# First block of each second pass: two products ahead of the last scores, the others in the usual order; joined with a new division of the W_lin sums and an earlier load of the last stored sum

## The chip, the cores and the metric

One core of a Trainium2 chip runs the whole kernel. The metric is the device time of one execution in microseconds (us), lower is better. The engines are TensorE (PE in the profile; its weight loads are PEld), VectorE (DVE), ScalarE (ACT), GpSimd (POOL) and SyncE (SP), which issues most of the DMAs, one after the other in program order.

## The reference

A pre-normalised graph network of two layers on 128 graphs of 64 nodes with 768 features, all in float32, with a residual around it. Cut to what matters:

```
h = relu(layernorm(x))                        # x: 128 x 64 x 768, adj: 128 x 64 x 64
for l in range(2):
    u_left  = (h @ (h @ W_left[l].T).T)  / sqrt(768)      # per graph
    u_right = (h @ (h @ W_right[l].T).T) / sqrt(768)
    u = upper triangle and diagonal of u_left, lower triangle of u_right
    e = exp(u) * adj
    attention = e / (sum(e, axis=2) + 1e-10)
    h_lin = h @ W_lin[l].T + b_lin[l]
    ctx = attention @ h_lin
    h = relu((ctx - mean) / (std + 0.001) * ln_a[l] + ln_b[l])
out = x + h
```

## The kernel before

The 8192 tokens are kept transposed (`ht`: features on partitions). Each layer has two passes over all of them.

**Pass one** makes the scores. The products of a 768x768 weight with tokens are made by a fast scheme: 40 products (`PRODUCTS`, L705) in place of more plain ones, each of a sum of weight blocks (a tile `g`, a "form") with a sum of token blocks (also `g`, or `ht` itself). One product is eight matmuls of 128x256 on PE. It writes one of the PSUM banks C, D, X, Y, Z, V, and is then read with signs into the results m0, m1, m2: the first read into a result is an ACT copy (L925), the others are DVE additions (L248, L929; L248 is the helper `added`). The tokens go by superblocks (`SUPER`, 11 per layer), and the 40 products are repeated for each. POOL makes the token sums (L248, `g<-ht`, `g<-ht,g`) a few products ahead; PE waits where one is late. After the fourth product of a superblock stand the scores of the superblock before (`scores`, L743), 288 short matmuls. The weight sums of layer 1 are formed during layer 0, stored to DRAM (`form`) and loaded in layer 1 (L654, `g<-form`).

**The plan.** What other engines do beside the products is written into a plan of slots: `put(slot, f)` enters a function, `turn_of(slot)`, called twice per product, runs what is due. The order of the code is the order in each engine's queue, and so one late instruction holds up what stands behind it. Beside the last superblock runs `final`: it loads the nine blocks of W_lin, centres them over the outputs (sums on ACT L236, means on DVE L231 and L232, the subtraction on ACT L240), does the same with the bias (`bias`: L983, L991, L994, L995, L998), and forms the 17 further weight sums of pass two (`W_SUMS`, by `sums_n`), by turns on POOL and DVE.

**Pass two** makes h_lin in 16 blocks with 15 products each (`ORDER`, L1021), into the banks Z, V, X, Y. `fresh` takes a bank and for four of the products writes the bias into it first (an ACT copy, L1010), `multiply` is the product, and a bank is read into h_lin (`hl`) by ACT (L303) or DVE. Of the first block the products 0 and 1 stand ahead of the scores of the last superblock of pass one; 3 and 5 come directly behind these, and then the others of the block in their order. Then follow the context (attention times h_lin, L1063, into `aux`), and from it a tile `z` (ACT L1208, L1226) that is normalised and stored for the next layer (`z<-z`). Of layer 0 there are four `z` buffers.

**The joint of the layers.** Layer 1 loads rows of z (`x<-z`, L364), transposes them by way of `xb` and `h` in DRAM, and loads `ht<-h` (L371). Those loads, the stored weight sums and the scores' own transfers all pass SyncE's one queue.

Of the kernel before, what the change touches and what calls it, by code (L numbers as in the profile page):

```python
# [10 lines left out]
F32 = mybir.dt.float32  # L11
I32 = mybir.dt.int32
AF = mybir.ActivationFunctionType
# [4 lines left out]
def kernel(  # L18
# [12 lines left out]
    nc = tc.nc  # L31
# [35 lines left out]
    def put(slot, *fs):  # L67
        plan.setdefault(slot, []).extend(fs)
# [12 lines left out]
    def run(slot):  # L81
# [7 lines left out]
        if background:  # L89
# [2 lines left out]

    SRC = {"l": w_left, "r": w_right, "n": w_lin}
    RAW = {8: (0, 1), 12: (1, 1), 9: (2, 1), 13: (2, 0), 11: (0, 0), 6: (1, 0), 3: (0, 2), 10: (1, 2), 14: (2, 2)}
    W_SUMS = ((5, "+", 8, 12), (9, "+", 9, 8), (8, "+", 8, 13), (0, "+", 5, 13), (4, "+", 3, 10),
# [3 lines left out]

    T_SUMS = (("ta", "+", "B0", "B2"), ("u1", "-", "B3", "B2"), ("u2", "-", "u1", "B0"), ("u0", "-", "B5", "B4"),  # L100
              ("u3", "-", "B1", "u0"), ("td", "+", "B3", "B4"), ("tb", "-", "B5", "B1"), ("te", "-", "B0", "u3"),
# [78 lines left out]
    def begins(k, l=0):  # L180
        return 0 if k == 0 else 2 * (len(PRODUCTS) if l else PLAIN) + 2 * len(PRODUCTS) * (k - 1)
# [65 lines left out]
    def added(eng, o, sign, a, b):  # L247
        (eng.tensor_add if sign == "+" else eng.tensor_sub)(o, a, b)  # L248

    def sums_n(l):  # L250
        t = W[l, "n"]

        def one(n, o, s, a, b):
            if o not in t:
                t[o] = free.popleft()
            added((nc.gpsimd, nc.vector)[n % 2], t[o], s, t[a], t[b])

        return [lambda n=n, x=x: one(n, *x) for n, x in enumerate(W_SUMS)]

    def later(fs, apart):  # L260
        for f in fs:
# [396 lines left out]
    def pass_one(l, start, final):  # L658
        with tc.tile_pool(name=f"one{l}", bufs=2, reuse_waits="tile") as sp, \
# [200 lines left out]
            def prepare(b, slot, step=1):  # L860
                if (l, b) not in XR:
                    load_rows(l, b, sp)
                end = put_all(slot + 1, [f for f in transpose_rows(l, b, sp) if step > 1 or f is not None], 1)
                if b + 1 < NB and (l, b + 1) not in XR:
                    if l == 0 and b > 2:
                        put(end - 5, lambda: load_rows(l, b + 1, sp, (0,)))
                        put(end, lambda: load_rows(l, b + 1, sp, (1,)))
                    else:
                        put(end + (8 if b == 2 else 0), lambda: load_rows(l, b + 1, sp))
                for t in range(2):  # L870
                    p = 2 * b + t
                    k = where[p][0]
                    before = p - 6
                    at = end + 3 + t
                    lag = 22 if b > 2 else 30 if l else 16
                    if before >= 0:
                        at = max(at, begins(where[before][0] + 1, l) + 2 * SCORED + 3)
                    put(at, lambda p=p, hold=before >= 0: load_part(1, l, p, hold))
                    put_all(at + lag + 6 * t, affine_part(1, l, p))
                    follow.setdefault(k, []).append(at + lag + (7 + 6 * t if l else 0))  # L880
                    if len(follow[k]) == len(SUPER[k]):
                        tokens.ready[k] = max(follow[k])
# [67 lines left out]
                    f()  # L950
            steps = softmax(last)
            steps[0]()
            for i in (0, 1, 3, 5):
                LEAD[i] = fresh(l, i, (0, 1))
                if i < 2:
                    multiply(l, 0, i, LEAD[i], (0, 1))
            scores(last)
            for i in (3, 5):
                multiply(l, 0, i, LEAD[i], (0, 1))
            for f in steps[1:4]:  # L960
                f()
            put_all(6, steps[4:], 3)
# [7 lines left out]
    def bias(l):  # L970


        ab = [free.popleft() for _ in range(2)]
        W[l, "bias"] = ab
        t = rows["bias", l] = [ab[n // 2][:, n % 2, :] for n in range(4)]
        todo = [lambda i=i, to=to: row(f"b{i}", b_lin[l], i * D, (i + 1) * D, t[to]) for i, to in enumerate((1, 2, 0))]
        bm = stat.tile([P, 3], F32, name="bm", bufs=1)

        bs = stat.tile([P, 1], F32, name="bs", bufs=1)

        def sums():
            for n in range(3):
                nc.scalar.activation(t[n], t[n], AF.Copy, accum_out=bm[:, n:n + 1])  # L983

        def mean():
            nc.vector.reduce_sum(bs, bm, axis=mybir.AxisListType.X)
            nc.vector.tensor_scalar_mul(bs, bs, -1.0 / H)

        def centred():
            for n in range(3):  # L990
                nc.scalar.activation(t[n], t[n], AF.Identity, bias=bs)  # L991

        def combined():
            nc.gpsimd.tensor_add(t[1], t[1], t[0])  # L994
            nc.gpsimd.tensor_add(t[3], t[1], t[2])  # L995

        def negated(n):
            nc.scalar.activation(t[n], t[n], AF.Copy, scale=-1.0)  # L998

        return todo, [sums, mean, centred, combined, lambda: negated(0), lambda: negated(2)]  # L1000
# [26 lines left out]
    def pass_two(l, aside):  # L1027
        last = l == L - 1
        with tc.tile_pool(name=f"two{l}", bufs=2, reuse_waits="tile") as sp, \
                tc.tile_pool(name=f"ps_two{l}", bufs=2, space=bass.MemoryType.PSUM, reuse_waits="tile") as ps_aux:  # L1030
            if last:
                for name, src in (("a", ln_a), ("b", ln_b)):
                    row(name, src[l], 0, H, sp.tile([P, H], F32, name=name, bufs=1))
            else:
                places(sp, {"hl": ([P, Q, H], 2), "at": ([P, Q, S], 2), "x": ([P, 2, H], 2),
                            "xb": ([P, H // 32, Q, 32], 1), "z": ([P, H], 4)}, ("hl", "at", "x", "xb", "z"))
            AT, HL = {}, {}
            if not last:
                extra = []
# [110 lines left out]
            def finish_block(u, more):  # L1150

                parts = context_block(u)
                tiles = ((0, 0), (0, 1), (1, 0), (1, 1))
                zs = {t: sp.tile([P, H], F32, name="z", bufs=4) for t in tiles}
                cut = (slice(0, T), slice(T, H))

                for t in ((1, 1), (1, 0)):
                    nc.vector.tensor_copy(zs[t][:, cut[0]], parts[t][0])
                    parts[t][0] = zs[t][:, cut[0]]
                    if t == (1, 1):  # L1160
                        AHEAD.append(fresh(l, 0, more))
                ss = stat.tile([P, Q, 2], F32, name="ssb", bufs=2)
                sd = stat.tile([P, Q], F32, name="sdb", bufs=2)
                rs = stat.tile([P, Q], F32, name="rsb", bufs=2)

                def squares(t):
                    junk = zs[0, t[1]]
                    for n in range(2):
                        nc.scalar.activation(junk[:, cut[n]], parts[t][n], AF.Square,
                                             accum_out=ss[:, 2 * t[0] + t[1], n:n + 1])  # L1170

                def deviation():
                    nc.vector.reduce_sum(sd, ss, axis=mybir.AxisListType.X)
                    nc.scalar.activation(sd, sd, AF.Sqrt, bias=floor, scale=1.0 / (H - 1.0))

                def inverse():
                    nc.vector.tensor_scalar_add(rs, sd, EPS_LN)
                    nc.vector.reciprocal(rs, rs)

                def scaled(t):  # L1180
                    by = rs[:, 2 * t[0] + t[1]:2 * t[0] + t[1] + 1]
                    for n in range(2):
                        nc.scalar.activation(zs[t][:, cut[n]], parts[t][n], AF.Copy, scale=by)
                    kept(u, *t, zs[t])

                order = ((1, 1), (1, 0), (0, 0), (0, 1))
                for f, slots in ((squares, (25, 26, 28, 29)), (scaled, (33, 34, 35, 36))):
                    for n, t in zip(slots, order):
                        put(n, lambda f=f, t=t: f(t))
                put(30, deviation)  # L1190
                put(32, inverse)
# [5 lines left out]
            def finish(u, r):  # L1197

                cx = context(u, r)
                zs = [sp.tile([P, H], F32, name="z", bufs=4) for _ in range(2)]  # L1200
                if last and not u and not r:
                    residual(u, r)
                two = "p (n d) -> p n d"
# [121 lines left out]
    def final_of(l):  # L1325
        def final(slot, tokens):
            put_all(slot + 6, load_n(l), 2)
            put(slot + 12, lambda: load_h(2, l, 0))

            def rest():  # L1330
                loads, work = bias(l)
                put_all(slot + 29, loads, 1)
                put_all(slot + 40, work, 4)

            put(slot + 28, rest)
            put_all(slot + 24, affine(2, l, 0), 2)
            put_all(slot + 28, centre(l), 1)
            for n, f in enumerate(sums_n(l)):
                put(slot + 42 + 3 * n // 2, f)
            put_sums_t((2, l, 0), slot + 56, 2, slot + 50)  # L1340
        return final

# [37 lines left out]
```

## Time and profile before

| | |
|---|---|
| median of 3 runs | 2643.37 us (2641.82 to 2644.38) |
| profiled execution | 2643.98 us |
| its span | 2642.2 us, 1.8 less |
| mean granted clock of PE | 0.996 |
| busy: PE, DVE, POOL, ACT | 98%, 67%, 67%, 35% |

The span is what the trace covers; all times of the trace count from its start. A row of the timeline has the start in us, the duration, engine, line, operation, the output and inputs by the program's names, and, in brackets, how long the engine sat idle just before and what ended that. A row of the stretches has start and end, then the busy time of each engine with its count of instructions, the granted clock of PE, the DMA share and the GB/s. Layer 0's pass one ends at about 860 us, layer 1's first pass begins at about 1330 and its second at about 2160.

### The profile page before, as it was taken

To read this page: it belongs to the slowest core of one execution; us is meant where nothing else is said; L and a number is where in the kernel's file an instruction comes from. 1 tells how busy PE (TensorE), PEld (TensorE's weight loads), DVE (VectorE), ACT (ScalarE), POOL (GpSimd) and SP (SyncE) were. 2 spreads that over 40 slices of the span, in tenths; PEclk is the share of its full clock that TensorE was granted. 3 is DMA by queue.
4 is the path that set the end of the run, shared out by engine and by line. 5 is a ranking of instruction groups with operands and counts; after the bars stand their busy time and mean duration, and the time that the engine had idled before them with its cause. 6 is when DMAs were issued, how large, how long until landed. Compare 5 with 4: busy or idle time off the path is not lost.

```text
span 2642.2 us, 47249 instructions
## 1 busy us (share of the span) xinstructions
PE 2590.5 (98%) x18122; PEld 2216.3 (84%) x18122; DVE 1776.0 (67%) x2884; ACT 934.9 (35%) x1969; POOL 1764.3 (67%) x1396
## 2 busy tenths in 40 slices
PE   9899999999999999999999999999999999999998
PEld 8788888888888888888788888888888878887886
DVE  6878787777768445454456677677766676666667
ACT  5522223223113344454542222222222335555453
POOL 4766676666668657676176666667666657878786
PEclk9999999999999999999999999999999999999999
DMA  7534434333421354445794524353542215555555
GB/s 219 115 109 98 113 93 125 92 106 79 98 57 60 123 164 142 159 144 183 218 279 96 126 59 113 76 129 93 131 104 70 66 50 160 156 166 167 176 161 146
DMA packets 258465, 331.84 MB, mean 126 GB/s; under 512 B 56002, under 2 KB 190402, under 8 KB 258242
## 3 DMA queue, kind: packets, MB, share of 16 engines
q1 hardware_dynamic: 241442, 320.56, 44.2%
q10 hardware_dynamic: 16800, 8.26, 1.2%
q8 instruction: 145, 2.38, 0.4%
q14 instruction: 78, 0.64, 0.1%
HBM read 213.39 MB, written 115.34 MB: 124 GB/s over the span
## 4 chain that ended last, share of the span: by engine, by line
PE 86%; DVE 5%; DMA 3%; ACT 2%; issue 1%; POOL 1%; SPq 1%; ACTq 0%; DVEq 0%; POOLq 0%
PE Z L1021 12%; PE C L705 8%; PE Y L705 8%; PE X L705 8%; PE D L705 8%; PE Y L1021 8%; PE Z L705 8%; PE V L705 7%; PE X L1021 6%; PE sc L743 5%; PE V L1021 4%; PE aux L1063 2%; DVE m L248 2%; POOL g L248 1%; DMA g<-form 1%
## 5 line engine op out<-in xcount | busy, mean ns | idle before, releaser
L248 POOL TENSOR_TENSOR g<-ht 128x512 f32<-128x512 f32 (+1 forms) x620 | 785.1, 1277 | 410.5 <-PE X L705 74.4
L248 POOL TENSOR_TENSOR g<-g,g 128x512 f32<-128x512 f32 (+1 forms) x310 | 396.8, 1287 | 140.9 <-PE C L705 22.6
L248 POOL TENSOR_TENSOR g<-ht,g 128x512 f32<-128x512 f32 (+1 forms) x272 | 346.0, 1281 | 164.9 <-PE Z L705 44.1
L705 PE MATMUL C<-g,g 128*128 128x256 f32 x1008 | 243.9, 386 | 11.9 <-POOL g L248 6.6
L705 PE MATMUL X<-g,g 128*128 128x256 f32 (+1 forms) x1080 | 251.6, 376 | 2.6 <-DVE m L929 1.4
L1021 PE MATMUL Z<-g,g 128*128 128x256 f32 x1024 | 244.1, 380 | 2.9 <-ACT hl L303 2.7
L705 PE MATMUL Y<-g,g 128*128 128x256 f32 (+1 forms) x968 | 226.7, 377 | 4.4 <-POOL g L248 4.4
L705 PEld LDWEIGHTS C<-g,g 128*128 128x128 f32 x1008 | 193.6, 193 | 41.3 <-issue 7.1
L705 PEld LDWEIGHTS X<-g,g 128*128 128x128 f32 x1080 | 201.5, 190 | 31.5 <-POOL g L248 2.5
L382 ACT ACTIVATE ht<-ht,b_col,a_col 128x256 f32<-128x256 f32 x384 | 196.2, 592 | 70.8 <-DMA ht<-h 50.5
L1021 PEld LDWEIGHTS Z<-g,g 128*128 128x128 f32 x1024 | 191.6, 190 | 35.2 <-issue 4.1
L705 PE MATMUL Z<-g,g 128*128 128x256 f32 (+1 forms) x936 | 217.0, 375 | 0.0
L705 PE MATMUL D<-g,g 128*128 128x256 f32 x880 | 208.0, 379 | 0.5 <-POOL g L248 0.5
L705 PEld LDWEIGHTS Y<-g,g 128*128 128x128 f32 x968 | 182.9, 191 | 28.7 <-POOL g L248 4.8
L705 PE MATMUL V<-g,g 128*128 128x256 f32 (+1 forms) x840 | 194.1, 374 | 3.8 <-DMA g<-form 3.4
L705 PEld LDWEIGHTS Z<-g,g 128*128 128x128 f32 x936 | 174.5, 190 | 23.1
L705 PEld LDWEIGHTS D<-g,g 128*128 128x128 f32 x880 | 167.1, 190 | 24.0 <-POOL g L248 1.1
L1021 PE MATMUL X<-g,g 128*128 128x256 f32 x768 | 182.7, 379 | 0.0
L705 PEld LDWEIGHTS V<-g,g 128*128 128x128 f32 x840 | 157.0, 190 | 24.0 <-DVE m L248 3.7
L1221 POOL TENSOR_TENSOR z<-z,b 128x768 f32<-128x768 f32 x62 | 112.6, 1828 | 81.8 <-DVE z L1218 77.2
L248 DVE TENSOR_TENSOR m<-m,D 128x512 f32<-128x512 f32 x180 | 118.2, 677 | 72.4 <-ACT m L925 53.8
L248 DVE TENSOR_TENSOR m<-m,Y 128x512 f32<-128x512 f32 (+2 forms) x196 | 126.4, 667 | 59.4 <-ACT m L925 36.6
(222 smaller groups left out, 4604.4 us busy)
## 6 DMA issues: line engine op xcount, KB each, us to landing
ht<-h SPq DMA_DIRECT2D x126, 768.0 KB, 6.2
h<-xb SPq DMA_DIRECT2D x124, 384.0 KB, 6.6
z<-z SPq DMA_DIRECT2D x128, 192.0 KB, 3.1
x<-z SPq DMA_DIRECT2D x128, 192.0 KB, 5.5
xr<-in_x_dram SPq DMA_DIRECT2D x120, 192.0 KB, 3.9
out_dram<-xr SPq DMA_DIRECT2D x120, 192.0 KB, 2.7
x<-in_x_dram SPq DMA_DIRECT2D x112, 192.0 KB, 4.8
g<-form SPq DMA_DIRECT2D x40, 256.0 KB, 5.5
```

The lines of the kernel that those rows point to most:

```text
L248: (eng.tensor_add if sign == "+" else eng.tensor_sub)(o, a, b)
L382: nc.scalar.activation(ht, ht, AF.Relu, bias=cols[1][:, c:c + 1], scale=cols[0][:, c:c + 1])
L705: nc.tensor.matmul(o, w[:, c, g * P:(g + 1) * P], t, start=(new and g == c == at == 0), stop=(c == K2 - 1), skip_group_check=True)
L743: nc.tensor.matmul(p[h * S + e:h * S + e + 32, q, e:e + 95], ht[:, c, b * S + e:b * S + e + 32], mb[:, e:e + 95], start=new, stop=not left ...
L1021: nc.tensor.matmul(p[:, n], b[t][:, c, r * P:(r + 1) * P], w[s][:, c, :], start=(i in FIRST and i not in PRELOAD and n == c == 0), stop=(c ...
L1063: nc.tensor.matmul(cx[k][i, m, :HH], at[j, q, :], hl[j, q, m * HH:(m + 1) * HH], start=True, stop=True)
L1221: nc.gpsimd.tensor_add(zs[k], zs[k], rows["b"])
```

## The change

The first part: of the first block of pass two only the products 0 and 1 are made ahead of the order, and 3 and 5 come in their places among the others.

```diff
-            for i in (0, 1, 3, 5):
+            for i in (0, 1):
                 LEAD[i] = fresh(l, i, (0, 1))
-                if i < 2:
-                    multiply(l, 0, i, LEAD[i], (0, 1))
+                multiply(l, 0, i, LEAD[i], (0, 1))
             scores(last)
-            for i in (3, 5):
-                multiply(l, 0, i, LEAD[i], (0, 1))
```

TensorE's queue, end of pass one of layer 0 (`sc` is the scores' bank, the rows without it are products of pass two, with bank, token sum and weight). Before:

```order
475 L1021 MATMUL V<-g_119,g_143 128x256 x4
480 L743 MATMUL sc<-m_288,ht 32x95 x48
481 L1021 MATMUL X<-g_123,g_140 128x256 x4
482 L1021 MATMUL Y<-g_147,ht 128x256 x4
483 L1021 MATMUL Z<-g_135,g_121 128x256 x4
484 L1021 MATMUL Z<-g_153,ht 128x256 x4
485 L1021 MATMUL Z<-g_132,g_160 128x256 x4
486 L1021 MATMUL X<-g_163,g_118 128x256 x4
```

And now:

```order
475 L1036 MATMUL V<-g_119,g_157 128x256 x4
480 L755 MATMUL sc<-m_288,ht 32x95 x48
481 L1036 MATMUL Z<-g_154,g_121 128x256 x4
482 L1036 MATMUL X<-g_132,g_140 128x256 x4
483 L1036 MATMUL Z<-g_153,ht 128x256 x4
484 L1036 MATMUL Y<-g_147,ht 128x256 x4
485 L1036 MATMUL Z<-g_127,g_160 128x256 x4
486 L1036 MATMUL X<-g_143,g_118 128x256 x4
```

X and Y, which stood ahead of three products into Z, now stand between them. (Names of buffers differ, since the pool hands them out in another order; the token and weight blocks are the same.)

The second part: the sums of the W_lin blocks have slots of their own; 11 are on POOL ("g") and 6 on DVE ("v"). Those of DVE have one operand in PSUM ("a", "b"), which ACT copies there, into the bank of the scores. Likewise ACT writes two centred rows of the bias into bank V too, and the two additions move from POOL to DVE.

```diff
-    W_SUMS = ((5, "+", 8, 12), (9, "+", 9, 8), (8, "+", 8, 13), (0, "+", 5, 13), (4, "+", 3, 10),
...
-            for n, f in enumerate(sums_n(l)):
-                put(slot + 42 + 3 * n // 2, f)
+            put_sums_n(l, slot)
...
+    N_SUMS = ((37, "g", 5, "+", 8, 12), (37, "v", 9, "+", "a", 8), (43, "g", 8, "+", 8, 13), (45, "g", 0, "+", 5, 13),
+              (47, "g", 11, "+", 11, 13), (50, "g", 7, "+", 6, 10), (51, "v", 2, "-", 9, "a"),
...
+    N_COPIES = ((35, "a", 9), (40, "b", 9), (49, "a", 14))
+
+    def put_sums_n(l, slot):
         t = W[l, "n"]
-
-        def one(n, o, s, a, b):
+        banks = {n: KEEP["scores"][:, i].rearrange("p (c d) -> p c d", c=K2) for i, n in enumerate("ab")}
+
+        def copy(o, s):
+            nc.scalar.copy(banks[o], t[s])
+
+        def one(eng, o, s, a, b):
             if o not in t:
                 t[o] = free.popleft()
-            added((nc.gpsimd, nc.vector)[n % 2], t[o], s, t[a], t[b])
+            added({"g": nc.gpsimd, "v": nc.vector}[eng], t[o], s, *(banks[v] if v in banks else t[v] for v in (a, b)))
...
+        for n, *x in N_COPIES:
+            put(slot + n, lambda x=x: copy(*x))
+        for n, *x in N_SUMS:
+            put(slot + n, lambda x=x: one(*x))
...
+        bank = KEEP["V"]
+
         def centred():
+            for n in range(2):
+                nc.scalar.activation(bank[:, n * D:(n + 1) * D], t[2 * n], AF.Identity, bias=bs)
             for n in range(3):
                 nc.scalar.activation(t[n], t[n], AF.Identity, bias=bs)
 
         def combined():
-            nc.gpsimd.tensor_add(t[1], t[1], t[0])
-            nc.gpsimd.tensor_add(t[3], t[1], t[2])
+            nc.vector.tensor_add(t[1], t[1], bank[:, :D])
+            nc.vector.tensor_add(t[3], t[1], bank[:, D:])
```

POOL's queue in the last superblock of layer 0, where the first W_lin sum stands (`g30<-g5,g39` before, `g9<-g5,g39` now; rows with `ht` and the rows between are token sums). Before:

```order
417 L248 TENSOR_TENSOR g9_123<-ht_5357,g15_129 128x512
418 L248 TENSOR_TENSOR g13_127<-ht_5308,ht_5357 128x512
419 L248 TENSOR_TENSOR g29_143<-g38_152,g7_121 128x512
420 L248 TENSOR_TENSOR g43_157<-g41_155,g7_121 128x512
421 L248 TENSOR_TENSOR g30_144<-g5_119,g39_153 128x512
422 L248 TENSOR_TENSOR g46_160<-ht_5364,ht_5357 128x512
```

And now:

```order
417 L244 TENSOR_TENSOR g9_123<-g5_119,g39_153 128x512
418 L244 TENSOR_TENSOR g13_127<-ht_5357,g15_129 128x512
419 L244 TENSOR_TENSOR g29_143<-ht_5308,ht_5357 128x512
420 L244 TENSOR_TENSOR g43_157<-g38_152,g7_121 128x512
421 L244 TENSOR_TENSOR g30_144<-g41_155,g7_121 128x512
422 L244 TENSOR_TENSOR g46_160<-ht_5364,ht_5357 128x512
```

The first W_lin sum has moved ahead of four token sums.

The third part: in layer 1 too the loads of rows come in halves, the rows of block 3 and the second load of tokens of block 2 get slots of their own, and layer 0's pass two has six z buffers.

```diff
-                    if l == 0 and b > 2:
-                        put(end - 5, lambda: load_rows(l, b + 1, sp, (0,)))
+                    if b > 2:
+                        put(end - (3 if l else 5), lambda: load_rows(l, b + 1, sp, (0,)))
                         put(end, lambda: load_rows(l, b + 1, sp, (1,)))
                     else:
-                        put(end + (8 if b == 2 else 0), lambda: load_rows(l, b + 1, sp))
+                        put(72 if l else end + 8, lambda: load_rows(l, b + 1, sp))
...
+                    if (l, b, t) == (1, 2, 1):
+                        at, lag = begins(1, l) + 2 * SCORED + 4, 10
...
-                zs = [sp.tile([P, H], F32, name="z", bufs=4) for _ in range(2)]
+                zs = [sp.tile([P, H], F32, name="z", bufs=4 if last else 6) for _ in range(2)]
```

SyncE's queue at the start of pass one of layer 1 (`form_39` is the last stored weight sum, `z_3` rows of block 3, `h1_5` tokens). Before:

```order
367 L371 DMA ht_9401<-h1_4_201 128x1536
368 L371 DMA ht_9405<-h1_5_202 128x1536
369 L654 DMA g40_154<-form_36_110 128x512
370 L654 DMA g14_128<-form_37_111 128x512
371 L654 DMA g47_161<-form_38_112 128x512
372 L364 DMA x_9427<-z_3_232 32x2x768 x4
373 L364 DMA x_9432<-z_3_232 32x2x768 x4
374 L654 DMA g38_152<-form_39_113 128x512
```

And now:

```order
367 L383 DMA ht_9406<-h1_4_201 128x1536
368 L666 DMA g21_135<-form_36_110 128x512
369 L666 DMA g14_128<-form_37_111 128x512
370 L666 DMA g47_161<-form_38_112 128x512
371 L666 DMA g38_152<-form_39_113 128x512
372 L376 DMA x_9588<-z_3_232 32x2x768 x4
373 L376 DMA x_9593<-z_3_232 32x2x768 x4
374 L383 DMA ht_9776<-h1_5_202 128x1536
```

The last stored sum has moved ahead of the eight row loads, and the second load of tokens behind them.

More of the change, by code (lines that the diff above doesn't have):

```diff
@@ L248, in added @@
         (eng.tensor_add if sign == "+" else eng.tensor_sub)(o, a, b)
-    def sums_n(l):
+    N_SUMS = ((37, "g", 5, "+", 8, 12), (37, "v", 9, "+", "a", 8), (43, "g", 8, "+", 8, 13), (45, "g", 0, "+", 5, 13),
[4 rows of a table added]
+    N_COPIES = ((35, "a", 9), (40, "b", 9), (49, "a", 14))
+    def put_sums_n(l, slot):
         t = W[l, "n"]
-        def one(n, o, s, a, b):
+        banks = {n: KEEP["scores"][:, i].rearrange("p (c d) -> p c d", c=K2) for i, n in enumerate("ab")}
+        def copy(o, s):
+            nc.scalar.copy(banks[o], t[s])
+        def one(eng, o, s, a, b):
             if o not in t:
                 t[o] = free.popleft()
-            added((nc.gpsimd, nc.vector)[n % 2], t[o], s, t[a], t[b])
-        return [lambda n=n, x=x: one(n, *x) for n, x in enumerate(W_SUMS)]
+            added({"g": nc.gpsimd, "v": nc.vector}[eng], t[o], s, *(banks[v] if v in banks else t[v] for v in (a, b)))
[3 more added lines that the diff above has]
+            put(slot + n, lambda x=x: one(*x))
     def later(fs, apart):
@@ L1035, in pass_two @@
                 places(sp, {"hl": ([P, Q, H], 2), "at": ([P, Q, S], 2), "x": ([P, 2, H], 2),
-                            "xb": ([P, H // 32, Q, 32], 1), "z": ([P, H], 4)}, ("hl", "at", "x", "xb", "z"))
+                            "xb": ([P, H // 32, Q, 32], 1), "z": ([P, H], 6)}, ("hl", "at", "x", "xb", "z"))
             AT, HL = {}, {}
@@ L1153, in finish_block @@
                 tiles = ((0, 0), (0, 1), (1, 0), (1, 1))
-                zs = {t: sp.tile([P, H], F32, name="z", bufs=4) for t in tiles}
+                zs = {t: sp.tile([P, H], F32, name="z", bufs=6) for t in tiles}
                 cut = (slice(0, T), slice(T, H))
```

6 rows, old and new, of tables (N_SUMS, W_SUMS) are left out of this document.

## The prediction

> **What bounds the kernel now.** I read the page first, then the idle time of TensorE along the span, and then, at each gap, the engines that it waits for. The page:
>
> ```profile
> span 2642.2 us, 47249 instructions
> PE 2590.5 (98%) x18122; PEld 2216.3 (84%) x18122; DVE 1776.0 (67%) x2884; ACT 934.9 (35%) x1969; POOL 1764.3 (67%) x1396
> ```
>
> TensorE is busy for 2590.5 us of 2642.2. The change removes none of its work (its products are the same, in another order at two places), so the only thing to win is idle time and half-clock time of PE, in the four places that the change touches: the end of pass one of layer 0 and of layer 1 (about 800 to 850 and 2100 to 2150 us), the first block of each second pass (870 and 2170), the joint of the layers (1300 to 1390), and the steady part of layer 1. These are TensorE's rows of the timeline there; the third column group is the idle time just before and what ended it:
>
> ```profile
> 835.79 1.95 PE L705 MATMUL Y<-ht,g 128*128 128x256 f32 x8
> 840.26 3.55 PE L705 MATMUL C<-g,g 128*128 128x256 f32 x8 [2.52 <-POOL g L248]
> 843.65 1.68 PE L705 MATMUL D<-g,g 128*128 128x256 f32 x7
> ...
> 2130.14 1.99 PE L705 MATMUL D<-ht,g 128*128 128x256 f32 x8
> ...
> 2138.74 1.97 PE L705 MATMUL C<-g,g 128*128 128x256 f32 x8 [2.52 <-DVE m L248]
> 2142.27 1.89 PE L705 MATMUL X<-g,g 128*128 128x256 f32 x8
> 2143.99 1.89 PE L705 MATMUL Y<-g,g 128*128 128x256 f32 x8
> 2146.46 1.97 PE L705 MATMUL C<-g,g 128*128 128x256 f32 x8 [0.58 <-DVE m L248]
> ...
> 871.62 1.99 PE L1021 MATMUL Z<-g,ht 128*128 128x256 f32 x8 [0.69 <-ACT hl L303]
> 874.39 1.96 PE L1021 MATMUL Z<-g,g 128*128 128x256 f32 x8 [0.78 <-ACT hl L303]
> 876.20 1.89 PE L1021 MATMUL X<-g,g 128*128 128x256 f32 x8
> ...
> 2173.29 1.97 PE L1021 MATMUL Z<-g,g 128*128 128x256 f32 x8 [0.78 <-ACT hl L303]
> ...
> 1383.76 1.39 PE L705 MATMUL Z<-g,g 128*128 128x176 f32 x8
> 1388.59 1.71 PE L705 MATMUL V<-g,g 128*128 128x176 f32 x8 [3.44 <-DMA g<-form]
> 1390.09 3.35 PE L705 MATMUL C<-g,g 128*128 128x256 f32 x8
> 1393.27 1.89 PE L705 MATMUL D<-g,g 128*128 128x256 f32 x8
> ```
>
> The pace of undisturbed products of 128x256 is 2143.99 - 2142.27 = 1.72 us, and I count what a start is later than this pace. Two products take twice their time (3.55 and 3.35 where others take 1.89). The granted clock says why:
>
> ```profile
> 840.10:843.40 3.30, 3.14 (x8) 2.54 (x9) 3.30 (x5) 0.00 (x0) 3.30 (x4) 0.50 0.00 0
> 1389.70:1393.00 3.30, 3.30 (x10) 2.75 (x9) 2.62 (x6) 0.00 (x0) 1.27 (x1) 0.50 0.00 0
> 2138.80:2142.20 3.40, 3.40 (x16) 3.01 (x17) 3.40 (x5) 0.00 (x0) 3.40 (x3) 1.00 0.00 0
> ```
>
> After the gaps at 840.26 and 1388.59 the clock was 0.50 (third number from the end) for one stretch of about 3.4 us, after the equally long gap at 2138.74 it stayed 1.00. A half-clock stretch costs half of itself, about 1.7 us.
>
> **The change part by part.**
>
> *Loads of layer 1 (start of its pass one).* The wait of 3.44 us is for the last stored weight sum. SyncE's own rows:
>
> ```profile
> 1369.53 2.49 SPq L654 DMA_DIRECT2D g<-form  x3
> 1372.07 10.42 SPq L364 DMA_DIRECT2D x<-z  x8
> 1382.95 0.34 SPq L654 DMA_DIRECT2D g<-form  x1
> g<-form SPq DMA_DIRECT2D x40, 256.0 KB, 5.5
> ```
>
> Its issue stands behind eight row loads that take 10.42 us, and it lands 5.5 us after 1382.95, at 1388.45. In the changed order it stands ahead of them, as a fourth of the group at 1369.53, so it is issued at about 1372 and lands at about 1378, where the product would want it at 1383.76 + 1.19 = 1384.95. Without wait V starts at 1384.95, C 1.19 later at 1386.14 and D at 1387.86; before, D started at 1393.27. That is 5.4, of which I leave 0.2 to the token sum that C needs: **5.2**, of which about 1.7 is the half clock. What is moved behind, the eight loads and the second load of tokens (`ht`), is wanted a superblock later; layer 0 already loads its rows by halves, so I give the steady part nothing. Bounds: 0 (another wait in its place) and 5.4.
>
> *First block of pass two.* 871.62 and 874.39 are products into bank Z that follow a product into Z and so wait until ScalarE has read the bank (`hl L303`). The idle times shown are 0.69 + 0.78 = 1.47; by the starts the second is 874.39 - 871.62 - 1.72 = 1.05 late, and in the same proportion the first 0.93, together 2.0. I take **1.8** per layer, between the two. In the changed order an X or Y product lies between two Z products, as from 876.20 on, where no wait is shown. Layer 1 has the same products and again 0.78 at 2173.29: 2 x 1.8 = **3.6**. The two bias copies for X and Y, which moved from ahead of the scores to behind them, lie beside the 6 us of scores. Bounds: 0, if a copy comes late for its product, and 3.6.
>
> *Sums of the W_lin blocks, layer 0.* The releaser printed at 840.26 is not the real one: DVE's own rows show its reads of the bank held up.
>
> ```profile
> 827.38 1.78 DVE L248 TENSOR_TENSOR g<-g,g 128x512 f32<-128x512 f32 x1
> 837.18 1.74 DVE L248 TENSOR_TENSOR g<-g,g 128x512 f32<-128x512 f32 x1 [1.49 <-POOL g L248]
> 838.84 1.27 DVE L248 TENSOR_TENSOR m<-m,C 128x512 f32<-128x512 f32 x2
> L248 DVE TENSOR_TENSOR g<-sc,g x7: 674/678/692, 26.0 to 90.9; 128x512 f32<-128x512 f32 x7
> L520 ACT COPY sc<-g x22: 575/590/593, 23.6 to 90.2; 128x512 f32<-128x512 f32 x22
> ```
>
> A W_lin sum waits 1.49 us on POOL and then takes 1.74; behind it the two reads of bank C end at 840.11, and C starts at 840.26. A sum with both operands in SBUF took 1.78 and 1.74; the same sum with one operand in PSUM (`sc`) took 0.678. In the changed order no sum stands between the reads of Y and of C, and the six that DVE keeps have a PSUM operand. So C comes 1.72 after Y, if nothing earlier is late. What the change adds is earlier:
>
> ```profile
> 814.23 1.28 POOL L248 TENSOR_TENSOR g<-g,g 128x512 f32<-128x512 f32 x1 [2.25 <-ACT g L240]
> 821.55 1.28 POOL L248 TENSOR_TENSOR g<-g,g 128x512 f32<-128x512 f32 x1 [3.57 <-ACT g L983]
> 816.38 1.89 PE L705 MATMUL C<-g,g 128*128 128x256 f32 x8
> 820.58 0.42 ACT L983 ACTIVATE g<-g 128x256 f32<-128x256 f32 x1 [0.77 <-DMA g<-in_b_lin_dram]
> 830.94 0.69 DVE L248 TENSOR_TENSOR m<-m,D 128x512 f32<-128x512 f32 x1 [1.18 <-ACT m L925]
> 831.92 1.89 PE L705 MATMUL D<-ht,g 128*128 128x256 f32 x8
> ```
>
> POOL's first W_lin sum now stands four token sums earlier, but cannot start before ScalarE has centred its block, at 814.2. So the token sums behind it follow from there: the one that the product at 816.38 needs ends at 814.2 + 2 x 1.25 = 816.7 to 816.8, and PE waits 0.3 to 0.5; one more such place gives another 0.3. ScalarE gets five instructions more, 3 x 0.59 + 2 x 0.42 = 2.6 us; its wait of 0.77 for the bias load and, as I estimate, 0.3 of other idle time take up part, so its read of bank D comes 1.5 later, and with it DVE's, which waits for it (830.94 to 831.63), and the D product, which followed that by 0.3. D comes at about 833.4, X, Y and C at 1.72 each: C at 838.6, and the D after it at 840.3 instead of 843.65. That is **3.3** (3.4 - 0.1 of smaller waits), and it takes the half-clock stretch with it. Bounds: the whole 4.4 (843.65 against 835.79 + 2 x 1.72 = 839.23) with ScalarE's delay absorbed; and, with nothing absorbed and POOL's 0.8 on top, D at 835.3, C at 840.5 and the next D at 842.2, a gain of 1.4, or -0.3 if a half-clock stretch follows the gap ahead of D. I take 3.3, since the waits that absorb are rows of the trace.
>
> [...]
>
> *The same, layer 1.* There no bias load's wait takes up ScalarE's delay, so D (2130.14) comes 2.4 later, at 2132.6, and C, after X, Y at 1.72 and a small wait, at 2138.1: 0.6 ahead of 2138.74. The late start at 2146.46 (2143.99 + 1.72 = 2145.71, so 0.75), behind another long sum, goes too: **1.4**. Bounds: 0.5, if POOL's 0.8 adds to the delay (C at 2138.9), or -1.2 with a half-clock stretch behind the gap ahead of D; and 3.9 with D on time (C at 2135.6, 3.1, and the 0.75).
>
> *Six z buffers in pass two of layer 0.*
>
> ```profile
> 1311.20 0.81 ACT L1208 ACTIVATE z<-aux 128x768 f32<-128x768 f32 x1 [2.23 <-DMA z<-z]
> 1313.73 1.13 PE L1021 MATMUL Z<-g,g 128*128 128x256 f32 x4 [1.18 <-ACT hl L303]
> 1340.79 1.08 ACT L382 ACTIVATE ht<-ht,b_col,a_col 128x256 f32<-128x256 f32 x2
> 1354.84 1.46 PE L705 MATMUL X<-g,g 128*128 128x176 f32 x8 [0.93 <-DVE m L929]
> ```
>
> ScalarE waits until a z tile is stored, and PE waits behind it, 1.18; two more tiles take such waits away. ScalarE's wait bounds this for one tile at 2.2, and I estimate at most 2.9 with the shorter waits that follow. But from 1340.79 on, ScalarE's work follows loads of tokens whose issue is not moved, and the products up to 1354.84 follow that; what PE wins it waits there again. I take **0**; bounds -1 and +2.9.
>
> **The sum**: 5.2 + 3.6 + 3.3 + 1.4 + 0 = 13.5. The profiled execution took 2643.98 us (span 2642.2 and 1.8 around it; the median of the runs is 2643.37, 0.6 less). 2643.98 - 13.5 = **2630.5**. About 0.2% (5.3 us) is what a measurement can tell from no change.
>
> **The rivals.**
>
> 1. *ScalarE's delay eats the ends of pass one.* Five more instructions on the engine for which POOL waits three times there (2.25 and 3.57 above), and C is as late as before. For it: the D read has no slack. Against: 1.5 and 2.4 late is less than the gap. Only 5.2 + 3.6 = 8.8 is left: 2635.2. Chance 0.15.
> 2. *The load is early, and PE waits for something else at 1385,* a token sum on POOL or the next token load: 13.5 - 5.2 = 8.3, 2635.7. For it: the order of token loads changes there too. Against: the product behind, C, started without a wait once V was done. Chance 0.08; with rival 1 both, 2640.4, no difference: 0.06.
> 3. *The z gain is kept* because row loads also come earlier: 2627.6. Chance 0.10.
> 4. *The clock stretch does not go with its gap,* or another falls elsewhere: 1.7 less per place, 2632.2 or, for both, 2633.9. Chance 0.10.
> 5. *Slower: POOL's waits become PE's.* In before POOL sat out 2.25 + 3.57 = 5.8 us waiting for ScalarE, with token sums done ahead. The first W_lin sum now holds up four of these. If 5.8 us fell on PE in both layers, with a half-clock stretch each, the ends of pass one would lose 11.6 + 3.4 = 15.0, and 15.0 - 8.8 = 6.2 slower: 2650.2. It decides where ScalarE's centring ends over 5.3 us later than 814.2 in both layers ((8.8 + 5.3 - 3.4) / 2). Against: ahead of it ScalarE gets only one of the five instructions. Chance 0.08.
>
> **How the numbers follow.** My forecast as worked out has 0.43. Faster by over 0.2% (below 2638.7): 0.43 + 0.15 + 0.08 + 0.10 + 0.10 = 0.86; same 0.06; slower 0.08. The range runs from 2625 (19.0 of the 5.4 + 3.6 + 4.4 + 3.9 + 2.9 = 20.2 that all upper bounds give) to 2638 (6.0, below rivals 1 and 2 with 8.8 and 8.3, for their smaller bounds); outside lie the cases of no change and slower, 0.14, and some 0.05 at the ends.
>
> **What would show it.** Right: no wait on the stored sum near 1388 and clock 1.00 there; no pairs of 0.69 and 0.78 in the first block of pass two; DVE's `g<-sc,g` near 0.68; the C product near 840 following Y at pace; D about 1.5 late at 833. Wrong: a new wait of PE on POOL at 815 to 830 of more than 1 us, or a D product over 3 us late, or a half-clock stretch that has no gap.

## The result, and the profile after

| | before | after |
|---|---|---|
| median of 20 runs | 2642.03 us (2637.86 to 2644.58) | 2633.9 us (2631.29 to 2641.0) |
| ratio | | 0.9972, 95% interval 0.9966 to 0.9978 |
| profiled execution, its span | 2643.98, 2642.2 us | 2636.03, 2634.2 us |

The changed kernel is 0.28% faster (0.22% to 0.34%), 7 to 8 us; the forecast was 13.5, in the right direction and with a time within its range, and it was too much by 5 to 6. Three of the five terms came out short, the sums of layer 0 by the most. TensorE's rows of the changed kernel, at the places that the prediction showed (its line 717 is 705 of before, 1036 is 1021, 755 is 743):

```profile
814.13 1.89 PE L717 MATMUL Y<-g,g 128*128 128x256 f32 x8
816.28 1.99 PE L717 MATMUL C<-g,g 128*128 128x256 f32 x8 [0.27 <-POOL g L244]
...
834.66 2.89 PE L717 MATMUL D<-ht,g 128*128 128x256 f32 x8 [2.32 <-DVE m L244]
837.35 2.72 PE L717 MATMUL X<-g,g 128*128 128x256 f32 x8
839.90 1.89 PE L717 MATMUL Y<-ht,g 128*128 128x256 f32 x8
841.63 1.89 PE L717 MATMUL C<-g,g 128*128 128x256 f32 x8
843.36 1.89 PE L717 MATMUL D<-g,g 128*128 128x256 f32 x8
...
872.36 1.89 PE L1036 MATMUL Z<-g,g 128*128 128x256 f32 x8
874.08 1.89 PE L1036 MATMUL X<-g,g 128*128 128x256 f32 x8
...
1313.20 1.13 PE L1036 MATMUL Z<-g,ht 128*128 128x256 f32 x4 [0.69 <-ACT hl L315]
1340.17 1.43 PE L717 MATMUL Y<-g,g 128*128 128x176 f32 x8 [1.09 <-POOL g L244]
1344.99 1.43 PE L717 MATMUL V<-g,g 128*128 128x176 f32 x8 [1.63 <-POOL g L244]
...
1382.96 1.36 PE L717 MATMUL V<-g,g 128*128 128x176 f32 x8
1384.16 1.89 PE L717 MATMUL C<-g,g 128*128 128x256 f32 x8
1385.88 1.89 PE L717 MATMUL D<-g,g 128*128 128x256 f32 x8
...
2106.85 1.89 PE L717 MATMUL Y<-g,g 128*128 128x256 f32 x8
2109.55 1.99 PE L717 MATMUL C<-g,g 128*128 128x256 f32 x8 [0.81 <-POOL g L244]
2127.02 1.99 PE L717 MATMUL D<-ht,g 128*128 128x256 f32 x8 [1.42 <-DVE m L244]
2139.53 1.89 PE L717 MATMUL C<-g,g 128*128 128x256 f32 x8
2158.43 1.97 PE L1036 MATMUL Z<-g,g 128*128 128x256 f32 x8 [0.83 <-ACT hl L315]
```

And the rows of before that these are set against, which were not shown yet:

```profile
814.65 1.89 PE L705 MATMUL Y<-g,g 128*128 128x256 f32 x8
2112.73 1.89 PE L705 MATMUL Y<-g,g 128*128 128x256 f32 x8
```

The same product's start in both gives how far PE is ahead: 0.52 us at the Y product near 814; 0.29 at D (843.65 against 843.36); 2.12 at the X product of the first block (876.20 against 874.08); 2.13 at V (1347.12 against 1344.99); 7.39 at D (1393.27 against 1385.88); 5.88 at Y near 2110; 6.93 at C (2146.46 against 2139.53); 7.95 at the end of the span, since nothing but the first block of layer 1 still differs. So the profile gives, term by term:

| term | forecast | between the two profiles |
|---|---|---|
| load of the last stored sum | 5.2 | 5.3 |
| first block of pass two, layers 0 and 1 | 3.6 | 1.8 + 1.0 |
| sums, end of pass one of layer 0 | 3.3 | -0.2 |
| sums, end of pass one of layer 1 | 1.4 | 1.05 |
| six z buffers | 0 | 0.0 |
| elsewhere (start, and scores of layer 1) | 0 | -1.0 |

"Elsewhere" is 0.5 won ahead of 814 and 1.5 lost between 1393 and 2110. At 814 the profiles of the experiments below stand between 2.6 us ahead of the kernel before and 1.4 behind. Between 1410 and 2100 PE's only idle times of length are gaps among the scores, the longest of 1.20 us, that the trace puts down to nothing ("issue"); they add up to 3.8 us here, to 2.2 before, and to 0.9 to 3.2 in the experiments, with the third part and without it. So neither is shown to be an effect of the change.

The gap of layer 0 did not go: it moved from product C to product D, with a half-clock stretch behind it (the product at 834.66 takes 2.89 and the next 2.72; from 835.7 to 839.1 the granted clock is 0.51). What PE waits for there stands in the rows of ScalarE and DVE:

```profile
827.62 2.20 ACTq L690 DMA_DIRECT2D adj<-in_adj_dram  x2
829.87 0.91 ACT L236 ACTIVATE g<-g,wmm 128x256 f32<-128x256 f32 x2 [1.96 <-DMA adj<-in_adj_dram]
830.69 0.97 ACT L1004 ACTIVATE V<-g,bs 128x256 f32<-128x256 f32 x2
831.59 1.29 ACT L1006 ACTIVATE g<-g,bs 128x256 f32<-128x256 f32 x3
832.79 0.57 ACT L260 COPY sc<-g 128x512 f32<-128x512 f32 x1
833.30 0.58 ACT L939 ACTIVATE m<-D 128x512 f32<-128x512 f32 x1
...
833.92 0.69 DVE L244 TENSOR_TENSOR m<-m,D 128x512 f32<-128x512 f32 x1 [5.82 <-ACT m L939]
834.52 0.68 DVE L244 TENSOR_TENSOR g<-g,sc 128x512 f32<-128x512 f32 x1
```

ScalarE issues four loads of adjacency itself; the issue of the last two takes 2.20 us of its queue, and ScalarE sits idle for 1.96 of them. Behind that stand the bias rows for bank V, the bias, the third copy into PSUM, and only then the read of bank D, at 833.30 where it was at 830.34. DVE sits idle for 5.82 us for it, and PE for 2.32. The W_lin sum behind it takes 0.68, as forecast.

### The profile page after: what moved, and what is told of

It is laid out like the page before. It is cut to its first block, busy times and chain, and to the rows that moved or that the text cites. A ratio compares the mean times of both kernels' runs of the same rounds, so it can differ in the third digit from the quotient of the medians.

```text
span 2634.2 us, 47267 instructions
## 1 busy us (share of the span) xinstructions
PE 2589.2 (98%) x18122; PEld 2215.5 (84%) x18122; DVE 1764.7 (67%) x2884; ACT 940.0 (36%) x1979; POOL 1762.7 (67%) x1396
## 4 chain that ended last, share of the span: by engine, by line
PE 89%; DVE 4%; ACT 3%; DMA 2%; issue 1%; SPq 1%; POOL 0%; ACTq 0%; DVEq 0%; POOLq 0%
PE Z L1036 12%; PE Y L717 9%; PE X L717 9%; PE C L717 9%; PE D L717 8%; PE Y L1036 8%; PE Z L717 8%; PE V L717 8%; PE X L1036 6%; PE sc L755 5%; PE V L1036 4%; PE aux L1078 2%; DVE m L244 2%; PE aux L1101 1%; DVE st L351 1%
```

## The experiments

Two theories stood against each other. *Theory 1*: each part does what its own place in the trace shows; the second part wins next to nothing, since its five instructions on ScalarE, and the four loads that ScalarE issues, stand ahead of the read of bank D. *Theory 2*, the forecast: the second part wins its 4.7, and what lacks was lost elsewhere.

**The parts by themselves.** The first part alone is the first piece of the diff put into the kernel before, without the others.

> The kernel before with the first part alone (the order of the first block of pass two). Theory 1 (each part does in the changed kernel what its own place in the trace shows): the two waits of 0.69 and 0.78 go in both layers, 2.0 us won in layer 0; in layer 1 about 1.0, since the first Z product after the scores now waits for a read of bank Z that itself waits for the end of the scores (0.83 in the changed kernel). Together -3 us against before. Theory 2 (the forecast): -3.6 to -4, without a wait on the first Z product of layer 1.

Measured: 0.9984 (0.9975 to 0.9992), 4.2 us at the middle and 2.1 to 6.6 by the interval, which holds both theories. Its profile decides for the first: by the starts of the same products 2.0 us are won in layer 0 and 0.8 in layer 1, where the first Z product behind the scores waits 0.83 for ScalarE. The second part alone:

> The kernel before with the second part alone (the division of the W_lin sums, with the copies and bias rows in PSUM). Theory 1: about nothing, -1 to +1 us: the gap ahead of product C near 840 is gone, but a gap of about 2.4 us stands ahead of product D near 833, because ScalarE's read of bank D comes 2.5 to 3 us later; a half-clock stretch may follow that gap in layer 0 in one execution and not in the next (1.7 us). Theory 2 (the forecast): -3.3 - 1.4 = -4.7, and what was lacking in the changed kernel was lost in the scores between 400 and 1800 us.

Measured: 0.9996 (0.9988 to 1.0005), 1.1 us faster at the middle, with no difference and 3 us within the interval; 4.7 is outside it. Its D product:

```profile
834.23 1.99 PE L717 MATMUL D<-ht,g 128*128 128x256 f32 x8 [2.17 <-DVE m L244]
```

```profile
834.20:837.60 3.40, 3.37 (x14) 2.69 (x15) 3.37 (x7) 0.00 (x0) 3.40 (x4) 1.00 0.00 0
```

The gap is there as in the changed kernel, and in this execution the clock of that stretch (second fence, third number from the end) stayed 1.00. The third part alone:

> The kernel before with the third part alone (loads of layer 1 and six z buffers). Both theories: -5.3 us: no wait of PE on the last stored sum near 1388, clock 1.00 there; the waits of pass two's last block behind the stores of z are gone (about 2.7 us won by 1325) and as much is lost again between 1335 and 1350, to token sums on POOL. If the row loads by halves cost something in the steady part of layer 1 it is less than 5.

Measured: 0.9991 (0.9982 to 0.9999), 2.4 us, 0.3 to 4.8 by the interval. Its profile shows the gap near 1388 gone, but the time says less than 5.3; where the rest went is not shown. The three parts by themselves add up to 4.2 + 1.1 + 2.4 = 7.7 us, about what the changed kernel wins. Without the second part (first and third together):

> The changed kernel without its second part (W_lin sums and bias as before, order and loads as changed). Theory 1: as fast as the changed kernel, -8 us against before, with the gap ahead of product C near 840 back in both layers and no gap ahead of D. Theory 2: slower than the changed kernel by 4 to 5 us, -4 against before.

Measured: 0.9977 (0.9967 to 0.9987). The changed kernel had 0.9972 (0.9966 to 0.9978): the second part adds 1.3 us at the middle, which these runs do not tell from zero. This run's own interval, 3.4 to 8.7 us against before, holds both theories; it is the second part alone, at most 3.2 us, that excludes the 4.7 of theory 2. The two gaps ahead of product C are back here, and the clock behind them is the other way round from before:

```profile
839.30:842.70 3.40, 3.40 (x16) 3.01 (x17) 3.40 (x5) 0.00 (x0) 3.40 (x4) 1.00 0.00 0
2128.10:2131.50 3.40, 3.40 (x8) 2.72 (x9) 3.40 (x5) 0.00 (x0) 3.40 (x4) 0.51 0.00 0
```

**ScalarE's queue.** Both moves below touch only slots, in the last superblock of both layers:

```diff
-put(slot + 2 * SCORED + 42, lambda k=k: load_adj(k, nc.scalar))
+put(slot + 2 * SCORED + (46 if k == last else 42), lambda k=k: load_adj(k, nc.scalar))
```

This alone:

> The changed kernel with only the four adjacency loads issued by ScalarE moved behind the read of bank D. Theory 1: the waits of 1.96 and 1.04 on ScalarE ahead of the last centred block go, the read comes that much earlier, and the gaps ahead of the D products shrink from 2.32 and 1.42 to about 0.5 each; 2.8 us less than the changed kernel. Rival (only the five additional instructions count, the loads are issued beside other work): no change.

Measured: 0.9967 (0.9955 to 0.998), median 2632.13: by the time alone not told apart from the changed kernel (0.9972). What it shows is in its profile, below. Together with the rest of the bias work and the third copy behind the read (the two bias rows for bank V, and also the three instructions that centre the bias, which the kernel before had ahead of the read too):

```diff
-                put_all(slot + 40, work, 4)
+                put_all(slot + 40, work[:2], 4)
+                put_all(slot + 52, work[2:], 4)
...
-    N_COPIES = ((35, "a", 9), (40, "b", 9), (49, "a", 14))
+    N_COPIES = ((35, "a", 9), (40, "b", 9), (51, "a", 14))
...
-(51, "v", 2, "-", 9, "a")
+(53, "v", 2, "-", 9, "a")
```

> The changed kernel with ScalarE's read of bank D ahead of five of the things that stood before it: the four adjacency loads that ScalarE issues, the bias rows and the third copy into PSUM now stand behind it, in both layers. Theory 1 (ScalarE's additional and earlier work delays the read, which delays the D product): the read starts near 828.9 instead of 833.3, the gaps of 2.32 and 1.42 ahead of the D products are gone, none takes their place at product C, and PE is 2.5 + 1.6 = 4.1 us ahead of the changed kernel behind the ends of pass one, 1.7 more where a half-clock stretch goes. Rival (DVE's sums or POOL set the D product): the gaps stay, no change of time.

Measured: 0.9957 (0.9945 to 0.997), median 2629.47, by ratio 4.0 us less than the changed kernel, where 4.1 and up to 1.7 more were expected. Where only the loads are moved, the D product stands so in the timeline (and with the same 0.26 in layer 1):

```profile
834.44 1.99 PE L717 MATMUL D<-ht,g 128*128 128x256 f32 x8 [0.26 <-DVE m L244]
```

And with all of it moved:

```profile
832.37 1.89 PE L717 MATMUL C<-g,g 128*128 128x256 f32 x8
834.09 1.89 PE L717 MATMUL D<-ht,g 128*128 128x256 f32 x8
835.82 1.89 PE L717 MATMUL X<-g,g 128*128 128x256 f32 x8
837.54 1.89 PE L717 MATMUL Y<-ht,g 128*128 128x256 f32 x8
```

2.32, 0.26 and none: taking the loads away takes most of the gap, taking the other work away the rest. This does not make the loads the cause by themselves: the kernel before had them at the same place and no gap ahead of D. It takes both, the loads and the five instructions of the change ahead of the same read. The read starts at 830.54 in the latter, later than the 828.9 expected, and still soon enough. The rival, that DVE's sums or POOL set the D product, is out.

**POOL's first W_lin sum.** On top of that, the first sum goes to slot 42, so that the token sums stand ahead of it again:

```diff
-((37, "g", 5, "+", 8, 12), (37, "v", 9, "+", "a", 8),
+((37, "v", 9, "+", "a", 8), (42, "g", 5, "+", 8, 12),
```

> As the one with ScalarE's read first, and POOL's first W_lin sum in slot 42 instead of 37, behind the token sums again. Theory 1: the waits of PE on POOL of 0.27 near 816 and 0.81 near 2109 go as well, 1.4 us less than without this. Rival (the sums behind it become late instead): new waits on POOL between 820 and 845 and no gain.

Measured: 0.9942 (0.9929 to 0.9954), median 2626.08, 3.4 us less than without it by the medians; the profiles show 2.0 for the two places together, and 1.4 was expected. No wait on POOL is left there:

```profile
812.13 1.89 PE L717 MATMUL Y<-g,g 128*128 128x256 f32 x8
813.86 1.89 PE L717 MATMUL C<-g,g 128*128 128x256 f32 x8
```

This is 15.3 us faster than before, by ratio; with the second part mended, the ends of pass one give 4.8 and 4.3 us in its profile, where the forecast had asked 3.3 and 1.4 of them.

**The z buffers.** The changed kernel with four:

> The changed kernel with four z buffers in pass two of layer 0 as before. Forecast: no change of time; the waits of 1.18, 0.81 and 1.49 near 1310 to 1325 come back (2.7 us), and the waits on POOL near 1340 and 1345 (1.09 and 1.63) shrink by as much. Rival: the stores' waits come back and POOL's waits stay, 2.7 us slower than the changed kernel.

Measured: 0.9972 (0.9961 to 0.9982), the same as the changed kernel. PE's waits there:

```profile
1311.85 1.13 PE L1036 MATMUL Z<-g,g 128*128 128x256 f32 x4 [1.07 <-ACT hl L315]
1314.66 1.13 PE L1036 MATMUL Z<-g,ht 128*128 128x256 f32 x4 [0.81 <-ACT hl L315]
1321.92 1.13 PE L1036 MATMUL Z<-g,ht 128*128 128x256 f32 x4 [1.09 <-ACT hl L315]
1344.87 1.43 PE L717 MATMUL V<-g,g 128*128 128x176 f32 x8 [0.42 <-issue]
```

With six buffers, in the rows of the changed kernel above, 0.69 at 1313.20 is the only one of length left of the first three, and the last, at 1344.99, is 1.63, with 1.09 ahead of it at 1340.17. For those two the profile names POOL, and so do the expectations, but the rows of ScalarE and DVE tell of another cause. With six buffers:

```profile
1339.13 0.60 ACT L394 ACTIVATE ht<-ht,b_col,a_col 128x256 f32<-128x256 f32 x1 [2.48 <-DMA ht<-h]
1339.97 4.03 ACT L394 ACTIVATE ht<-ht,b_col,a_col 128x256 f32<-128x256 f32 x8
1343.90 0.45 ACT L939 ACTIVATE m<-V 128x336 f32<-128x336 f32 x1
1344.38 0.51 DVE L244 TENSOR_TENSOR m<-m,V 128x336 f32<-128x336 f32 x1 [7.08 <-ACT m L939]
```

And with four:

```profile
1338.50 1.11 ACT L394 ACTIVATE ht<-ht,b_col,a_col 128x256 f32<-128x256 f32 x2
1344.26 0.51 DVE L244 TENSOR_TENSOR m<-m,V 128x336 f32<-128x336 f32 x1 [4.53 <-ACT m L939]
```

The product into bank V starts 0.10 us after DVE's read of this bank ends, with six buffers and with four (1344.89 and 1344.99, 1344.77 and 1344.87). This read stands behind ScalarE's, which stands behind its work on loaded tokens, and with six buffers ScalarE comes early and waits 2.48 us for that load. The load is issued at 1328.36 with six buffers and at 1328.19 with four: what PE wins earlier it waits there again. Four buffers in the kernel with the later first sum:

> As the one with ScalarE's read first and POOL's first W_lin sum later, with four z buffers. As between the changed kernel and its form with four z buffers, no difference: 2.6 us lost by 1325 to ScalarE's waits on stores, and as much not lost to POOL between 1335 and 1345. With six buffers PE there waited 2.40 and 1.63 on POOL in one go after the other; if such gaps bring half-clock stretches, four buffers are up to 1.7 faster.

Measured: 0.9936 (0.9923 to 0.9948), median 2624.95: the fastest by its median, but not told apart from 0.9942 with six. In the profile with six the products from 1333.88 to 1342, behind the waits of 2.40 and 1.63, take 1.43 and 1.91; in this one, with four, those from 1335 to 1343 take 1.36 to 1.91. Neither has a half-clock stretch there, and whether such waits bring one in other executions these two do not show.

**The first Z product of layer 1.** In the changed kernel it waits 0.83 for a read of bank Z that could not start until the scores were done:

```profile
2157.68 0.60 ACT L315 ACTIVATE hl<-Z 128x512 f32<-128x512 f32 x1 [15.14 <-PE sc L755]
```

> As the one with ScalarE's read first and POOL's first W_lin sum later; besides, in layer 1's first block of pass two each Z product changes places with the X or Y product behind it, so that an X product follows the scores, and the bias copy for X stands ahead of the scores. Theory 1: the wait of 0.83 on the first Z product of layer 1 is gone (1.07 by the starts) and no other comes; 1 us less than without this. Rival (any first product there waits for ScalarE): the X product waits as long.

Measured: 0.9959 (0.9945 to 0.9973), median 2630.57, so 4.5 us slower than without it. The X product directly follows the scores without a wait, as expected, but three others come:

```profile
2150.84 1.99 PE L1038 MATMUL Y<-g,ht 128*128 128x256 f32 x8 [1.17 <-ACT Y L1027]
2159.18 1.99 PE L1038 MATMUL Y<-g,ht 128*128 128x256 f32 x8 [1.18 <-ACT Y L1027]
2164.28 1.99 PE L1038 MATMUL Z<-g,g 128*128 128x256 f32 x8 [1.38 <-DVE hl L244]
```

The bias copies for the products 5 and 9 stand in the code behind the products 2 and 6. With each Z product behind its neighbour, these copies come directly ahead of the products that need them, and PE waits for them. The third is a Z product, 10, directly behind a Z product, 8, as in the kernel before, and waits for the read of the bank. The wait of 0.83 is gone, and more than four times as much has come for it (1.17 + 1.18 + 1.38).

**The moved loads by themselves.** A first try to have only the two lines that bring the stored sum forward:

> The kernel before with two lines of the third part alone: the rows of block 3 and the second load of tokens of block 2 in their new slots, so that the last stored sum is loaded ahead of them; row loads of layer 1 whole as before, four z buffers. Theory 1: the wait of 3.44 near 1388 is gone, -3.6, and up to -1.7 more as far as a half-clock stretch had followed that gap in the executions of before. Rival (the whole third part measured only -2.4 since the moved loads cost something in the steady part of layer 1): waits on row loads or tokens between 1400 and 2100, and less than -3.

Measured: 1.0266 (1.0252 to 1.028). The edit was wrong for its question: the slot that was meant for the rows of block 3 also took all later row loads of layer 1. It was past by then, so each block's rows were loaded only when their transposes began, and 12 blocks a second time at the end of pass one. Late rows and doubled loads together cost 70 us. The mended edit:

```diff
-put(end + (8 if b == 2 else 0), lambda: load_rows(l, b + 1, sp))
+put(72 if l and b == 2 else end + (8 if b == 2 else 0), lambda: load_rows(l, b + 1, sp))
...
+                    if (l, b, t) == (1, 2, 1):
+                        at, lag = begins(1, l) + 2 * SCORED + 4, 10
```

> The kernel before with the rows of block 3 and the second load of tokens of block 2 in their new slots, and all other row loads of layer 1 as before (in the run before this one, all later row loads had gone to a slot that was past: they came only when their transposes wanted them, and 12 blocks were loaded a second time at the end of pass one). Theory 1: the wait of 3.44 near 1388 is gone, without new waits between 1400 and 2100: -3.6, and up to -1.7 more as far as a half-clock stretch had followed that gap. Rival (what the whole third part lacked is the cost of the moved loads): less than -2, with a wait on rows or tokens of block 2 or 3 behind 1390.

Measured: 0.9986 (0.9977 to 0.9995), 3.7 us, 1.3 to 6.1 by the interval. V follows Z at pace, and D takes 1.89, where products in half-clock stretches took 2.72 to 3.65:

```profile
1384.21 1.39 PE L705 MATMUL Z<-g,g 128*128 128x176 f32 x8
1385.43 1.36 PE L705 MATMUL V<-g,g 128*128 128x176 f32 x8
1386.63 1.89 PE L705 MATMUL C<-g,g 128*128 128x256 f32 x8
1388.36 1.89 PE L705 MATMUL D<-g,g 128*128 128x256 f32 x8
```

That is the idle time of 3.44, and the intervals do not say whether the 1.7 of the half clock belongs to it too. Between this and the third part as a whole (2.4) no difference is shown.

## Why the prediction was right, and where it was short

*The number*: 2633.9 lies within 2625 to 2638 since the range was drawn wide enough for rivals 1 and 2, not since the sum was right. Rival 1's time, 2635.2, is nearer to the profiled 2636.03 than the forecast's 2630.5, and its mechanism is what layer 0 shows.

*What bounds the kernel* held: PE's busy time stayed at 2590 (2589.2 after), and all of the gain is idle and half-clock time of PE.

*Loads of layer 1*: right in mechanism and, between the profiles, in size (5.2 and 5.3). Over many runs it is 3.7 for the moved loads by themselves, with an interval that holds 5.2, and 2.4 for the whole third part, with one that does not. Of the three profiled executions that have the gap, that of before has one half-clock stretch behind it, that of the first part alone two in a row, and that of the second part alone none (mean granted clock from 1380 to 1400: 0.91, 0.83 and 1.00); so a mean over runs need not hold 1.7 for it.

*First block of pass two*: right for layer 0 (1.8). For layer 1 the step that failed is "Layer 1 has the same products", and so twice 1.8. In the order of before, X and Y stood between the scores and the first Z product, and covered the 0.6 us of ScalarE's read of bank Z, which in layer 1 starts only when the scores end (2157.68); layer 0 has no such wait. I costed the two copies that move and not the read that loses its cover: 0.83 idle, and 1.0 was left of 1.8.

*Sums, layer 0*: the step that failed is "its wait of 0.77 for the bias load and, as I estimate, 0.3 of other idle time take up part": ScalarE's read of D came 3.0 later, not 1.5. The wait of 0.77 for the bias did go, but others grew by 1.9 together: two waits for DVE near 819 and 826 from 0.76 and 0.49 to 1.45 and 0.78, and that on its own loads of adjacency from 1.05 to 1.96. That gap ahead of D was my lower bound "with nothing absorbed", with its half-clock stretch: -0.3 there, -0.2 in the trace. I should have counted the loads among what stands in ScalarE's queue. That the gap ahead of C would go, and that a sum with a PSUM operand takes 0.68, was right. The experiment that takes the cause away (2.32, 0.26, none) shows it. Rival 1 named this and gave it 0.15. The prediction's "A sum with both operands in SBUF took 1.78 and 1.74" leaves something out: in the kernel before two such sums of DVE, at 820.63 and 825.38, took 0.68 and 0.69, with POOL idle beside them, and the long ones ran beside a sum of POOL. So here the operand in PSUM is worth its 1.1 us only beside a sum of POOL.

*Sums, layer 1*: 1.05 of 1.4; D came 2.8 late against the Y product near 2110 (5.88 us ahead there, 3.12 at D, 2130.14 against 2127.02), where 2.4 was forecast; 0.8 of it is the wait on POOL.

*Six z buffers*: 0 was right, and so was the reason, ScalarE's work behind a load of tokens whose issue is not moved: PE comes to the product V at 1344.99 with six buffers and at 1344.87 with four, both times 0.10 behind DVE's read of the bank.

*The clock*: the prediction priced the stretches as tied to their gaps. The two 2.52 gaps of the kernel before had 0.50 and 1.00, those of the run without the second part 1.00 and 0.51, and the 2.17 and 2.32 gaps ahead of D 1.00 and 0.51. The length alone does not decide. From 800 to 860 the mean granted clock was 0.97 before, in the changed kernel, with the first part alone and with the third alone, and 1.00 with the second alone, behind its gap of 2.17; from 2100 to 2150 it was 1.00 in all five, behind the 2.52 of before too. What decides is not shown. So such a gap may bring the 1.7 or not, and in a mean over runs, as I estimate from the 0.50 and 1.00 behind equal gaps, it costs a part of it. Here 2.52 was enough at one place and not at another, so the measurement decides.

## What to carry to other kernels

Before work goes to an engine that looks idle (ScalarE, 35% busy), read its queue at the place where the bounding engine waits for it: what counts is the one read behind the new work, and DMA issues on that engine's own queue count as work (two took 2.20 us here, and ScalarE sat idle for 1.96). When products are put in another order, look also at which read had been covered by the products that are moved away (a wait of 0.83 here). A gap removed at one product can come back at another, as here 2.52 at C did as 2.32 at D; only the next late arrival tells what it is worth. And where the profile names an engine for a wait, see whether another instruction ended just before the product's start (here DVE's read of bank V, 0.10 us before).

## What the hardware showed that was not expected

Two DMA issues on ScalarE's queue took 2.20 us and kept it idle for 1.96, and moving four such issues behind one read took 2.06 off a gap of 2.32. And gaps of 2.52 us at the same product, with the same code there, had a granted clock of 0.50 or 0.51 behind them in one execution and 1.00 in another: in layer 0 0.50 before and 1.00 in the run without the second part, in layer 1 1.00 and 0.51. What tells them apart is not shown.
